# Layer 1's first eight columns of logits and v set among layer 0's last folds, and its contractions three columns later

## The chip, the cores and the metric

The kernel runs on one core of one Trainium2 chip. Its time is the device time of one execution, in microseconds (us); three runs are given for the kernel before. A profile is one more execution, recorded by the hardware profiler. The engines are TensorE (PE: matmuls; PEld: the loads of their stationary operand), VectorE (DVE), ScalarE (ACT), GpSimd (POOL) and SyncE (SP). SP computes nothing here and issues most transfers (DMAs); POOL and ACT issue some too. Every engine works through its instructions in the order in which the program lists them.

## The reference

Input x is [8, 56, 56, 384] in f32. Two layers follow one another, each of the form x = x + conv(gn(x)), where gn is a group norm with 32 groups without learned weights.

- Layer 0: v = gn(x) Wv. Each pixel has for each of 12 heads a 9 x 9 matrix of logits, a = gn(x) Wa, a softmax over its last axis, and with it makes 9 outputs out of the 3 x 3 neighbourhood of v; these are scattered back onto the 3 x 3 neighbourhood and added, and Wo is applied.
- Layer 1: logits gn(x) W_attn + b_attn (6 heads x 9), a softmax over the 9, v = gn(x) W_v + b_v, the weighted sum of the 3 x 3 neighbourhood of v, and W_proj with b_proj.

```
    y = jnp.einsum('bpKhd,bphK->bphd', patches, a)
    return y.reshape(B, H, W, C) @ W_proj + b_proj
```

## The kernel before

**Tiling.** Two images make a pair (4 pairs); a column is one x coordinate of a pair, 2 x 56 = 112 rows, with 384 channels. A pair has 56 columns, so layer 0 has 224 column steps. The 56 columns are cut into 8 patches of 7 columns (`PX = 7`, px in the names). In layer 1 a patch of a pair is a "group" g, 32 of them. Normalised tokens (xn) are held eight columns at a time. As 8 x 112 tokens are 7 tiles of 128, one column step in eight computes no logits.

**Layer 0** (`layer0`, L426). Step by step, `attend` (L611) makes a column's logits (three matmul groups `bank<-wa_t,xn`) and v (`bank<-wv_t,xn`). DVE subtracts the maximum, ACT takes the exponential; `normalise` (L684) and `presum` (L697) on POOL scale and partly sum the weights; `keep_v` (L640) has POOL store v to a table in DRAM (vtab). `fold` (L732), four steps later (`LAG`), finishes the sums with shift matmuls (`pw`), ACT and DVE writing them into four buffers (wts), and SP writes them to a weight table in DRAM (ztab). When a patch is complete, `fetch_v` and `fetch_z` read back v as vp and the weights as z in banded form, and `plan` (L800) enters jobs: contractions `pc<-z,vp` (two images, four parts each), evicted by ACT into yT, and six output projections `po<-yT,wo_t`. DVE adds the residual (x1t) and takes statistics of it; SP stores x1t to DRAM (x). Several jobs share one buffer po, so that a po directly behind another waits for DVE's addition.

**Layer 1** (`layer1`, L1015) does the like: `load` (L1036) fetches a group's x1t into one of five buffers (wide, z), `normed` (L1049) is ACT's normalisation into xn, `attend` (L1086) makes logits and v at once (`bank<-wc_t,xn`, 438 wide), added to their biases by DVE (lgt, v); its `store` has POOL write lgt to the group's tile at, and v to vtab. In the next group's columns, `weigh` (L1120) at column 3, `share` (L1128) at column 4 and `move` (L1136) at column 5 make the softmax on DVE and ACT, three shift matmuls (`pw<-at,shift`), ACT's copies and a write to ztab. `fetch` (L1172) reads z and vp and enters the group's jobs: contractions, and six po with DVE's addition of the residual and a transpose, and the output's DMAs.

**Order.** It is written out by hand. A `Jobs` queue (L358) holds (due step, job); every column step of either layer runs at most two of its jobs, one ahead of and one behind the step's matmuls. The last four steps of layer 0's loop (224 to 227) have only folds and jobs. The layer-1 loop (L1242) counts its own steps from `base`, the step at which layer 0's loop ended; at its step 0, `last` (L997) fetches and plans layer 0's last patch. `fetch` of group g - 2 stands at column 0 of group g, its jobs due three steps later.

**Buffers.** Layer 0's tiles (xr, xt, xin, xn, wa_t, wv_t and others) are in pools that are given up when `layer0` returns; layer 1's pools are laid over them, so that the first write to one of these waits for what last used that place. Layer 1's weights wc_t (L1070), loaded on POOL's queue, are such a tile.

Of the kernel before, what the change touches and what calls it, by code (L numbers as in the profile page):

```python
# [8 lines left out]
F32 = mybir.dt.float32  # L9
# [6 lines left out]
def two_outlook_layers(  # L16
# [80 lines left out]
    NTAB0, NTAB1 = 2, 3  # L97

# [327 lines left out]
    def layer0(late, pools):  # L426

        late_w = late.enter_context(tc.tile_pool(name="late0", bufs=1))
        io = pools.enter_context(tc.tile_pool(name="io0", bufs=2))
        work = pools.enter_context(tc.tile_pool(name="work0", bufs=2))  # L430
        fixed = pools.enter_context(tc.tile_pool(name="fixed0", bufs=1))
# [3 lines left out]
        def block_tile(pair, blk):  # L435
            t = io.tile([P, XB * NCH * R], F32, tag="xt", name=f"xt_{pair}_{blk}")
            return t[:, : XB * NCH * R].rearrange("p (m i r) -> p m i r", m=XB, i=NCH)
# [5 lines left out]
        xr_bufs = [io.tile([P, XB * C], F32, tag=f"xr{n}", name=f"xr_{n}", bufs=1) for n in range(2)]  # L443
# [6 lines left out]
        wts = fixed.tile([P, NWT, E0 * HEADS0 * PX], F32, name="wts0")  # L450
        xns = [fixed.tile([P, NCH, NTILE, P], F32, name=f"xn0_{n}") for n in range(2)]
# [34 lines left out]
        def blocks_in(flat, n, at=0):  # L486
# [14 lines left out]
            io.tile([P, XB, NCH, R], F32, tag="xin", name="xin_2", bufs=1),  # L501
# [22 lines left out]
        for blk in range(NBLK):  # L524
            if blk + NXR - 1 < NBLK:
                first_load(blk + NXR - 1)
            for i in range(NCH):
                for _ in stats_chunk(0, blk, i):
                    pass
            if blk == 1:  # L530
                wv_t = fixed.tile([P, NCH, C], F32, name="wv0_t")
                rows_of_channels(wv_t, wv0, sync)
# [29 lines left out]
        wa_t = fixed.tile([P, NCH, K * NL], F32, name="wa0_t")  # L562
# [15 lines left out]
        def load(g):  # L578
            pair, blk = divmod(g, NBLK)
            xins[g] = io.tile([P, XB, NCH, R], F32, tag="xin", name=f"xin_{g}", bufs=1)  # L580
            sync.dma_start(
                xins[g], xTs[pair][:, blk * XB : (blk + 1) * XB]
            )
# [345 lines left out]
        LAG = 4  # L929
        for step in range(NPAIR * W + LAG):  # L930
            folding = fold(*divmod(step - LAG, W)) if step >= LAG else iter(())
            turning = turned(step)
            summing = []

            def weigh():

                normal = 1 <= step < NPAIR * W + 1 and (step - 1) % SB < NTILE
                if 2 <= step < NPAIR * W + 2:
                    summing.append(presum(*divmod(step - 2, W)))
                    next(summing[0])  # L940
                if normal:
                    normalise(*divmod(step - 1, W))
                if normal and step % SB == NTILE:
                    share_out(*divmod(step - 1, W))
                for part in summing:
                    next(part)
                if normal and step % SB < NTILE:
                    share_out(*divmod(step - 1, W))
                if normal:
                    keep_v(*divmod(step - 1, W))  # L950

            def between(n):

                if n == 0:
                    next(turning, None)
                    weigh()
                    jobs.run(step, 1)
                elif n == 1:
                    if step % SB != NTILE:
                        next(folding, None)  # L960
                    next(turning, None)
                elif n == 2:
                    jobs.run(step, 1)
                    norms.run(step, 1)
                else:
                    for part in summing:
                        next(part)
                    if step % SB == NTILE:
                        jobs.run(step, 1)
                        next(folding, None)  # L970
                    next(folding, None)

            if step < NPAIR * W:
                attend(*divmod(step, W), between)
                upkeep(step)
            else:
                for n in range(K + 1):
                    between(n)
            flush()

            for lag, read, b in ((0, fetch_v, 0), (1, fetch_z, 0), (2, fetch_v, 1), (3, fetch_z, 1)):
                pair, c = divmod(step - LAG - PX - lag, W)
                if pair >= 0 and c % PX == 0 and c // PX < NPX:
                    px = c // PX
                    read(pair, px, b)
                    if lag == 1:
                        final = pair == NPAIR - 1 and px - NPX
                        ends = {-3: (8, 9, 9, 10, 10, 11), -2: (6, 7, 7, 8, 8, 9)}.get(
                            final, (7, 7, 8, 8, 9, 10)
                        )  # L990
                        second = (5, 6) if final == -2 else (6, 6)
                        plan(
                            pair, px, (step + 4, step + 5), [step + n for n in second],
                            [step + n for n in ends],
                        )

        def last(due):  # L997
            for b in range(IMG):
# [3 lines left out]
                NPAIR - 1, NPX - 1, (due + 4, due + 5), (due + 8, due + 8), [due + 9 + n for n in range(6)]  # L1002
            )

        return step + 1, last, late_w
# [9 lines left out]
    def layer1(pools, base, last_of_layer0, late_w):  # L1015
        vector, scalar, sync = (InOrder(e) for e in (nc.vector, nc.scalar, nc.sync))
        io = pools.enter_context(tc.tile_pool(name="io1", bufs=2, reuse_waits="tile"))
        work = pools.enter_context(tc.tile_pool(name="work1", bufs=2, reuse_waits="tile"))
        fixed = pools.enter_context(tc.tile_pool(name="fixed1", bufs=1, reuse_waits="tile"))
# [10 lines left out]
        def wide(n, pool, tag):  # L1030
            if n not in wides:
                wides[n] = pool.tile([P, NCH * T + SPARE], F32, tag=tag, name=f"wide_{n}", bufs=1)
# [3 lines left out]
        def load(g, queue=sync):  # L1036
            pair, px = divmod(g, NPX)

            if g % 5 == 3:
                t = wide(3, late_w, "xres")  # L1040
            elif g % 5 == 4:
                t = halves[3]
            else:
                t = wide(g % 5, io, f"x1t{g % 5}")
# [20 lines left out]
        load(0, nc.gpsimd)  # L1065

        NW = SX1 * K * ROW1
        wzs = [fixed.tile([R, NW + PX + 1], F32, name=f"wz1_{n}") for n in range(2)]
        NC1 = NA1 + C
        wc_t = fixed.tile([P, NCH, NC1], F32, name="wc1_t")  # L1070
        rows_of_channels(wc_t[:, :, :NA1], wa1, nc.gpsimd)
        rows_of_channels(wc_t[:, :, NA1:], wv1, nc.gpsimd)

        xns = [fixed.tile([P, NCH, SB, R], F32, name=f"xn1_{n}") for n in range(2)]
        normed(0, 0, PX)

        wo_t = fixed.tile([P, NCH, C], F32, name="wo1_t")
        by = io.tile([P, NR * 4 * QC], F32, tag="ot", name="wo1_by")
        by = by[:, : NCH * C].rearrange("p (i n) -> p i n", i=NCH)
        nc.sync.dma_start(by, wo1.rearrange("(i p) n -> p i n", p=P))  # L1080
        for i in range(NCH):
            sort_columns(wo_t, by, i, nc.gpsimd.tensor_copy)
# [3 lines left out]
        def attend(g, m):  # L1086
# [9 lines left out]
            lg = work.tile([P, NA1], F32, tag="lgt", name=f"lgt_{col}", bufs=4)  # L1096
            vector.tensor_add(lg, pa[:, :NA1], ba_t)
            v = work.tile([P, C], F32, tag="v", name=f"v_1_{col}", bufs=5)
# [12 lines left out]

        def at_of(g):

            if g not in lgs:
                lgs[g] = work.tile([R, PX, K2, HEADS1], F32, tag="at", name=f"at_1_{g}")
            return lgs[g]
# [3 lines left out]
        def weigh(g):  # L1120

            at = lgs[g]
            mx = work.tile([R, PX, HEADS1], F32, tag="mx", name=f"mx1_{g}")
# [4 lines left out]
        def share(g):  # L1128

            at = lgs[g]  # L1130
            den = work.tile([R, PX, HEADS1], F32, tag="den", name=f"den1_{g}")
# [4 lines left out]
        def move(g):  # L1136
# [12 lines left out]
            wz = wzs[g % 2]  # L1149
# [22 lines left out]
        def fetch(g, due):  # L1172
# [34 lines left out]
            def project_out(half, j):  # L1207
# [9 lines left out]
                if j == 0:  # L1217
                    fetch.ot = io.tile([P, NR * 4 * QC], F32, tag="ot", name=f"ot_{g}_{half}")
# [21 lines left out]

        NG = NPAIR * NPX
        for step in range((NG + 1) * PX):  # L1242
            g, m = divmod(step, PX)

# [5 lines left out]
            if step == 0:  # L1250
                last_of_layer0(base + step)
            if step == 4:
                for wz in wzs:
                    nc.gpsimd.memset(wz, 0.0)
            if g and m == first:
                weigh(done)
            if g and m == second:
# [8 lines left out]
            if g and m == moved:  # L1266
# [5 lines left out]
            if m == 1 and g + 1 < NG:  # L1272
                load(g + 1)
            if g > 1 and m == 0:
                while not clear_bands.done:
                    jobs.run(None, 1)
                fetch(done - 1, base + step + 3)
            if last and m == 4:
                fetch_v(done, 0)
                fetch(done, base + step + 1)  # L1280
            elif 0 < g < NG and m == 5:
                fetch_v(done, 0)
# [3 lines left out]
    with ExitStack() as late:  # L1286
        with ExitStack() as pools:
            last_of_layer0 = layer0(late, pools)
        with ExitStack() as pools:
            layer1(pools, *last_of_layer0)  # L1290
# [38 lines left out]
```

## Time and profile before

| | us |
|---|---|
| median of 3 runs | 3188.24 |
| lowest, highest | 3183.09, 3190.77 |
| the profiled execution | 3187.7 |
| its span, first to last instruction | 3185.5 |
| mean granted clock of PE | 0.989 of full |
| PE busy | 3065.3 |
| DVE busy | 2084.8 |
| POOL busy | 1654.2 |
| ACT busy | 1005.2 |
| first matmul with wc_t (layer 1's first logits) | at 2091.8 |

Lines of the profile name a source line, an engine, an operation, and out<-in by the names in the program. A helper issues all matmuls (L128) and most other operations (L143), so that lines are told apart by their tiles. A group "at 128x972" has 128 partitions and 972 elements in each. "Idle before <- X" is time in which the engine had nothing to run, and the instruction that ended it. The granted clock is the share of full speed that PE got. Matmuls of f32 are listed as two entries each, so that three matmuls make x6.

### The profile page before, as it was taken

To read this page: it belongs to the slowest core of one execution; us is meant where nothing else is said; L and a number is where in the kernel's file an instruction comes from. 1 tells how busy PE (TensorE), PEld (TensorE's weight loads), DVE (VectorE), ACT (ScalarE), POOL (GpSimd) and SP (SyncE) were. 2 spreads that over 40 slices of the span, in tenths; PEclk is the share of its full clock that TensorE was granted. 3 is DMA by queue.
4 is the path that set the end of the run, shared out by engine and by line. 5 is a ranking of instruction groups with operands and counts; after the bars stand their busy time and mean duration, and the time that the engine had idled before them with its cause. 6 is when DMAs were issued, how large, how long until landed. Compare 5 with 4: busy or idle time off the path is not lost. (4 is left out here: it accounts for less than half of the span.)

```text
span 3185.5 us, 72855 instructions
## 1 busy us (share of the span) xinstructions
PE 3065.3 (96%) x27640; PEld 2093.4 (66%) x27640; DVE 2084.8 (65%) x4942; ACT 1005.2 (32%) x2422; POOL 1654.2 (52%) x2759
## 2 busy tenths in 40 slices
PE   6899999999999999999999999989999999999997
PEld 5667766777776677776776666645666565656655
DVE  5777777777777777777777777635454555555454
ACT  4333333343333334333333333222222222222221
POOL 2765665655556565656566566544334344434431
PEclk8999999999999999999999999999999999999999
DMA  9799987899997899988888987889899988989897
GB/s 303 225 306 319 307 273 260 300 296 300 325 311 235 275 305 303 314 280 286 280 250 262 309 275 247 286 279 242 219 230 246 234 235 228 251 222 241 233 236 154
DMA packets 619842, 850.86 MB, mean 267 GB/s; under 512 B 264926, under 2 KB 496562, under 8 KB 611170
## 3 DMA queue, kind: packets, MB, share of 16 engines
q1 hardware_dynamic: 522322, 711.31, 73.7%
q0 software_dynamic: 63824, 116.90, 11.8%
q10 hardware_dynamic: 33344, 17.98, 2.1%
q8 instruction: 218, 3.57, 0.5%
q14 instruction: 134, 1.10, 0.1%
HBM read 514.86 MB, written 322.17 MB: 263 GB/s over the span
## 5 line engine op out<-in xcount | busy, mean ns | idle before, releaser
L128 PE MATMUL bank<-wa_t,xn 128*128 128x288 f32 x3528 | 967.8, 411 | 15.7 <-ACT xn L143 10.3
L128 PE MATMUL po<-yT,wo_t 128*128 128x448 f32 (+1 forms) x2304 | 817.0, 497 | 26.5 <-DVE x1t L143 19.4
L143 POOL TENSOR_TENSOR at<-at,d 128x972 f32<-128x972 f32 x196 | 441.2, 2251 | 714.8 <-DVE d L143 387.7
L128 PEld LDWEIGHTS bank<-wa_t,xn 128*128 128x128 f32 x3528 | 647.7, 191 | 226.2 <-issue 17.6
L128 PEld LDWEIGHTS po<-yT,wo_t 128*128 128x128 f32 x2304 | 433.6, 191 | 328.7 <-issue 195.8
L143 ACT ACTIVATE at<-at 128x972 f32<-128x972 f32 (+1 forms) x228 | 215.3, 944 | 997.1 <-DVE at L143 992.3
L1104 POOL DMA_DIRECT2D at<-lgt x392 | 204.8, 526 | 591.9 <-DVE lgt L143 580.8
L143 DVE TENSOR_REDUCE mx<-bank 128x36 f32<-128x324 f32 x588 | 284.8, 484 | 311.2 <-PE bank L128 309.3
L128 PE MATMUL bank<-wc_t,xn 128*128 128x438 f32 x1176 | 478.8, 543 | 5.1 <-DMA wc_t<-in_wv 5.1
L143 ACT COPY yT<-pc 128x294 f32<-128x294 f32 (+2 forms) x512 | 198.5, 405 | 804.9 <-PE pc L128 803.5
L128 PE MATMUL bank<-wv_t,xn 128*128 128x384 f32 x1176 | 414.5, 489 | 0.0
L128 PEld LDWEIGHTS pc<-z,vp 121*32 121x32 f32 (+1 forms) x17664 | 337.6, 120 | 111.9 <-issue 69.2
L128 PE MATMUL pc<-z,vp 121*32 121x49 f32 (+1 forms) x17664 | 374.2, 218 | 23.2 <-DMA z<-ztab 7.9
L128 PEld LDWEIGHTS bank<-wc_t,xn 128*128 128x128 f32 x1176 | 215.6, 191 | 180.9 <-issue 167.8
L143 DVE TENSOR_TENSOR at<-bank,mx 128x324 f32<-128x324 f32 x588 | 291.5, 496 | 31.0
L128 PEld LDWEIGHTS bank<-wv_t,xn 128*128 128x128 f32 x1176 | 220.8, 190 | 132.0 <-issue 9.3
L143 POOL DMA_DIRECT2D vtab<-v x476 | 289.5, 612 | 12.2 <-issue 6.8
L143 POOL TENSOR_TENSOR pre<-at,at 112x108 f32<-112x108 f32 (+1 forms) x440 | 236.5, 538 | 85.0 <-DMA at<-at 36.2
L143 DVE TENSOR_TENSOR lgt<-bank,ba_t 128x54 f32<-128x54 f32 x196 | 42.0, 214 | 308.7 <-PE bank L128 308.7
L333 POOL DMA_DIRECT2D vtab<-v x392 | 211.6, 544 | 16.0 <-issue 7.8
L143 DVE SCALAR_TENSOR_TENSOR wide<-po,bo_t,wide 128x448 f32<-128x448 f32 (+1 forms) x156 | 97.5, 625 | 167.4 <-PE po L128 167.3
L143 ACT ACTIVATE wts<-pre,inside 112x48 f32<-112x48 f32 (+4 forms) x672 | 179.3, 358 | 78.1 <-DMA ztab<-wts 66.2
(111 smaller groups left out, 2816.9 us busy)
## 6 DMA issues: line engine op xcount, KB each, us to landing
z<-ztab SPq DMA_DIRECT2D x64, 2352.0 KB
vp<-vtab SPq DMA_DIRECT2D x64, 1536.0 KB
vp<-vtab SPq DMA_DIRECT2D x64, 945.0 KB
xres<-xT SPq DMA_DIRECT2D x32, 1176.0 KB
ztab<-wts SPq DMA_DIRECT2D x336, 110.2 KB
vtab<-v POOLq DMA_DIRECT2D x108, 336.0 KB, 6.6
xin<-xT SPq DMA_DIRECT2D x52, 672.0 KB
xr<-in_x SPq DMA_DIRECT2D x50, 672.0 KB
```

The lines of the kernel that those rows point to most:

```text
L128: tc.keep_in_program_order(nc.tensor.matmul(*args, **kwargs))
L143: return lambda *args, **kwargs: tc.keep_in_program_order(op(*args, **kwargs))
L333: queue.dma_start(bass.AP(table.tensor, table.offset + first, [*([line * step, count] for step, count in rows_of or ((1, rows),)), *([[(R ...
L1104: nc.gpsimd.dma_start(at_of(g_of)[row : row + n, m_of].rearrange("r k h -> r (k h)"), lg[lo : lo + n])
```

## The change

Layer 1 becomes a generator that layer 0 starts and steps. Its buffers are handed over by name: the large tiles of layer 0 become "homes" that outlive it, and layer 1's tiles are slices of these (wc_t and the tiles lgt, v and at in xt and xin and xr; xn in xn; x of group 0 in xr, of group 1 in wa_t; layer 1's projection weights in wv_t). 40 steps before layer 0's last column step, x of group 0 and wc_t are loaded on POOL's queue; 7 to 5 steps before it, group 0 is normalised. At the last column step and in the four steps after it, 2, 1, 2, 2 and 1 columns of layer 1 (steps 1 to 7 and 9; step 8 has none) are computed among the folds and jobs, each with its stores at the end of the step. Layer 1's own loop starts with its step 10 (`AHEAD`), there loads x of group 2 and the projection weights and plans layer 0's last patch one or two steps closer than before. All fetches and jobs of a group are made by `of, turn`, three columns (`BEHIND`) after the columns that made them before; weigh, share and move stay where they were. The loop is three steps longer at its end. Of the buffers of x, those of group 2 and of groups 3 and 4 change places, and x of group 3 is loaded at column 4.

```diff
+    AHEAD, BEHIND = 10, 3
...
-        io = pools.enter_context(tc.tile_pool(name="io0", bufs=2))
+        xr_home = late_w.tile([P, 2 * XB * C], F32, name="xr_home")
+        xt_homes = [late_w.tile([P, XB * NCH * R], F32, name=f"xt_{n}") for n in range(2)]
+        xin_home = late_w.tile([P, XB * NCH * R], F32, name="xin_home")
+        xn_homes = [late_w.tile([P, NCH * SB * R], F32, name=f"xn_{n}") for n in range(2)]
+        wa_home = late_w.tile([P, NCH * K * NL], F32, name="wa0_t")
+        wv_t = late_w.tile([P, NCH, C], F32, name="wv_t")
...
+        ahead = layer1((xr_home, xt_homes, xin_home, xn_homes, wa_home, wv_t), late_w)
+        last_step = NPAIR * W - 1
+        first_of = {last_step - 40: 1, last_step - 7: 1, last_step - 6: 1, last_step - 5: 1}
+        columns = {last_step: 2, last_step + 1: 1, last_step + 2: 2, last_step + 3: 2, last_step + 4: 1}
+        stores = []
         for step in range(NPAIR * W + LAG):
+            for _ in range(first_of.get(step, 0)):
+                next(ahead)
+            more = iter(range(columns.get(step, 0)))
...
                     jobs.run(step, 1)
+                    if next(more, None) is not None:
+                        stores.append(next(ahead))
...
                     for part in summing:
                         next(part)
+                    while stores:
+                        stores.pop(0)()
...
             plan(
-                NPAIR - 1, NPX - 1, (due + 4, due + 5), (due + 8, due + 8), [due + 9 + n for n in range(6)]
+                NPAIR - 1, NPX - 1, (due + 3, due + 4), (due + 6, due + 6),
+                [due + n for n in (7, 8, 8, 9, 9, 10)],
             )
...
-        wc_t = fixed.tile([P, NCH, NC1], F32, name="wc1_t")
+        wc_t = xt_homes[0][:, : NCH * NC1].rearrange("p (i n) -> p i n", i=NCH)
...
+        load(0, nc.gpsimd)
+        rows_of_channels(wc_t[:, :, :NA1], wa1, nc.gpsimd)
+        rows_of_channels(wc_t[:, :, NA1:], wv1, nc.gpsimd)
+        yield
+        for m0, m1 in ((0, 3), (3, 5), (5, PX)):
+            normed(0, m0, m1)
+            yield
+        load(1, nc.gpsimd)
+        for step in range(1, AHEAD):
+            if step % SB == 0:
+                continue
+            if step == PX - 1:
+                normed(1, 0, 3)
+            yield attend(*divmod(step, PX))
+        normed(1, 3, PX)
+
+        pools, base, last_of_layer0 = yield
...
+        base -= AHEAD
...
-        for step in range((NG + 1) * PX):
+        for step in range(AHEAD, (NG + 1) * PX + BEHIND):
             g, m = divmod(step, PX)
+            of, turn = divmod(step - BEHIND, PX)
...
-            if step == 0:
+            if step == AHEAD:
                 last_of_layer0(base + step)
+                load(2)
...
-            if g > 1 and m == 0:
-                while not clear_bands.done:
-                    jobs.run(None, 1)
-                fetch(done - 1, base + step + 3)
-            if last and m == 4:
-                fetch_v(done, 0)
-                fetch(done, base + step + 1)
-            elif 0 < g < NG and m == 5:
-                fetch_v(done, 0)
+            if of > 1 and turn == 0:
+                assert clear_bands.done
+                fetch(of - 2, base + step + 3)
+            if of == NG and turn == 4:
+                fetch_v(NG - 1, 0)
+                fetch(NG - 1, base + step + 1)
+            elif 0 < of < NG and turn == 5:
+                fetch_v(of - 1, 0)
```

## The prediction

> **What bounds the kernel now.** The page first: busy time by engine, and the slices of the span.
>
> ```profile
> PE 3065.3 (96%) x27640; PEld 2093.4 (66%) x27640; DVE 2084.8 (65%) x4942; ACT 1005.2 (32%) x2422; POOL 1654.2 (52%) x2759
> PE   6899999999999999999999999989999999999997
> DMA  9799987899997899988888987889899988989897
> ```
>
> TensorE (PE) is busy for 3065 of 3185.5 us, so no more than 120 us is to be had without taking matmuls away. The slices show where those are missing: the start, slice 26 (counted from 0: 2071 to 2150 us), the end. Next I asked for busy time by stretch (columns: length, PE, PEld, DVE, ACT, POOL busy, granted clock, DMA share, GB/s):
>
> ```profile
> 2044.00:2112.00 68.00, 46.91 (x588) 28.05 (x587) 21.34 (x58) 10.25 (x24) 24.26 (x49) 0.85 1.02 358
> 2112.00:2150.00 38.00, 37.28 (x386) 21.48 (x385) 15.66 (x40) 12.39 (x29) 27.17 (x39) 1.00 0.59 181
> 2150.00:2166.00 16.00, 12.27 (x105) 7.68 (x103) 7.77 (x20) 3.35 (x7) 5.27 (x11) 0.79 1.00 253
> 2260.00:3060.00 800.00, 796.70 (x6117) 481.89 (x6112) 415.70 (x722) 199.06 (x582) 319.79 (x605) 1.00 0.90 236
> ```
>
> In layer 1's steady stretch PE idles 3.3 us of 800: nothing is left there. Between the layers it idles 21.1 + 0.7 + 3.7 = **25.5 us** of 122, at a lowered clock in two of the three stretches. PE's timeline there (start, length, operation, count, idle before and what ended it):
>
> ```profile
> 2048.28 4.09 PE L128 MATMUL po<-yT,wo_t 128*128 128x448 f32 x6 [3.19 <-DVE x1t L143]
> 2053.08 2.52 PE L128 MATMUL po<-yT,wo_t 128*128 128x448 f32 x6 [0.31 <-DVE x1t L143]
> 2056.32 1.96 PE L128 MATMUL po<-yT,wo_t 128*128 128x336 f32 x6 [0.72 <-DVE x1t L143]
> ...
> 2067.94 1.04 PE L128 MATMUL pc<-z,vp 121*32 121x49 f32 x56 [2.12 <-issue]
> 2068.91 1.14 PE L128 MATMUL pw<-pre,shift 112*112 112x120 f32 x4
> 2075.16 4.21 PE L128 MATMUL pc<-z,vp 121*32 121x49 f32 x192 [5.11 <-DMA z<-ztab]
> 2080.98 2.52 PE L128 MATMUL po<-yT,wo_t 128*128 128x448 f32 x6 [1.61 <-ACT yT L143]
> 2084.22 2.52 PE L128 MATMUL po<-yT,wo_t 128*128 128x448 f32 x6 [0.72 <-DVE x1t L143]
> 2091.84 4.42 PE L128 MATMUL bank<-wc_t,xn 128*128 128x438 f32 x6 [5.10 <-DMA wc_t<-in_wv]
> ```
>
> Six matmuls po of 448 take 2.42 us elsewhere, here 4.09 after the 3.19 us wait: idle PE is slowed afterwards. Losses of this kind: po 1.67, pw 1.14-0.57, pc 4.21-2.80, bank 4.42-2.37, and at 2158 pc 2.81-1.61 and bank 4.03-2.47: together **8.5 us**. So the transition loses 25.5 + 8.5 = 34.0 us. The wait of 5.10 us has a long root, in the table of waits and in the chain that ended last:
>
> ```profile
> POOL wc_t L269 <- DMA wo_by<-in_wo: 23.4, 1, 23.4
> 2064.70 11.79 DMA ztab<-wts
> 2077.98 4.67 DMA wo_by<-in_wo
> 2083.63 8.08 DMA wc_t<-in_wv
> ```
>
> Layer 1's weights wc_t can only be loaded when layer 0's pools are given up, behind layer 0's last ztab write.
>
> **The end of the kernel**, same view of PE:
>
> ```profile
> 3150.48 2.76 PE L128 MATMUL pc<-z,vp 90*64 90x56 f32 x84 [1.15 <-DMA z<-ztab]
> 3157.26 4.66 PE L128 MATMUL pc<-z,vp 90*64 90x56 f32 x84 [4.03 <-DMA vp<-vtab]
> 3162.31 14.74 PE L128 MATMUL po<-yT,wo_t 128*128 128x448 f32 x36 [0.39 <-ACT yT L143]
> ```
>
> From the last logits (end 3116.7) to PE's end, 3177.05, it idles 7.5 us (0.30, 0.52, 0.71, 0.40, 1.15, 4.03, 0.39) and loses 1.9 + 2.6 us to the clock: 12.0 us.
>
> **The change, part by part.** The matmuls stay the same in number; only waits can differ.
>
> *Removed:* the 5.10 us wait for wc_t. Its loads (0.79 and 0.76 us of POOL issue), x of group 0 (0.58) and its normalisation go into layer 0. On POOL's queue they stand among normalise and presum in pair 2, where POOL idles 2.8 to 2.9 us in each step; the 16-element memset ahead of x waits for PE's last transpose of xr (ends 1459.2), and POOL reaches it at about 1459.9. Six ACT normalisations lie beside an ACT that is 32% busy. The 1.85 MB meet a DMA share near 0.88 instead of 1.02: 0 to 6 us (1.85 MB at 300 GB/s, all of it waited for); I take 0.3, since z is fetched well before its use there. x of group 1 goes to the old wa_t, behind layer 0's last wa_t matmul (2040.5): POOL waits for none of it, as its next operation starts at 2041.1 anyway, 0.7 us later with the issue.
>
> *Added between the folds:* eight columns of 2.37 us among po, pw and pc, 19.0 us of PE work ahead of the contraction that waits for z today. From the end of the first po of px 5 (2044.5), the changed PE order up to pc of px 6, second image, start to start: 8 columns x 2.3, 2 po x 2.25, 3 po x 1.7, 5 pw x 0.5, pc 2.8, gaps 0.72 + 2.12: 36.1, so 2080.6. Its z goes out behind x1t's store, after 3 of these columns, 2 po and 2 pw, near 2059 (2056.9 today), and took 18.2 us: 2077. The 5.11 wait and the 3.19 are covered, so are 1.61 and 0.31; so is the stretch at 2150 (statistics spread between contractions, z fetched three columns later). If the cover failed, the 5.1 us and its clock loss would be back.
>
> A rule against it: the Trainium skill, "DMA: Bandwidth & Descriptors", section "Issuing engines are not separate DMA queues", says transfers from every issuing engine share the same 16 engines and interleave. So POOL's stores slow SP's z: 8 columns of 27 KB logits and about 247 KB v are 2.2 MB, at 380 GB/s 5.8 us, and z would come at 2083, a wait of over 2 us. By the rows, though, x of group 0 (1176 KB, POOL, 2058.7) leaves exactly this stretch, and only some five of the eight stores are out before z lands: net about nothing. I take 0 and keep 4 (wait and clock) for the range.
>
> *Left or new in the transition:* po directly after po waits for x1t: 0.72 + twice (0.72+0.72+0.60) = 4.8. The 2.12 "issue" wait, kept. Two new waits: SP issues x of group 2 behind both z of px 7 (about 9.4 MB from 2082, at 380 GB/s it lands near 2108), and ACT's normalisation of it stands ahead of the eviction of pc of px 7, which PE reaches near 2107 (2080.6 + pc 2.8 + po 11.9 + gaps 2.0 + 4 columns 9.2 + pw 0.8); on POOL the 4.04 us memset of z stands ahead of stores of logits that DVE's maximum needs, ahead of x1t. Either costs 0 to 6; they delay the same work, so I take 3.0 for both. Clock: 1.0. Sum 10.9. **Transition: 34.0 - 10.9 = 23.1 us gained.**
>
> *Contractions three columns later, steady.* Fetches come five instead of two columns after the weights' write: more slack. Softmax on DVE now falls in the po columns. Worst group (a skipped column): share takes 0.83+0.42+0.55 = 1.8 us, then the third po's addition ends 9.0 us after the logits' end; PE needs that buffer at 11.5. Slack 2.5 us; cost 0. Bounds: -3 (all the idle time goes) to +1 us for each of 31 groups.
>
> *The end.* After the last logits PE has both contractions of group 29 (2 x 2.76 = 5.5), then the shift matmuls of group 31. These need: POOL's second issue at +1.2, landing 5.1, reduction to share 0.79+0.55+0.52+0.83+0.42+0.55, handovers 0.5: +10.5. A **new wait of about 5.0 us**, in PE's order ahead of po of group 29, which hid it before. After it z and vp of group 31 are issued about 12 us before use, as po of 30 lies between: the 1.15 + 4.03 go. What follows the new wait is slowed. The skill's "TensorE: Matmul & The Clock Gate", Part 1, lets the clock drop after about 3.4 us idle and return after as long: 1.7 us lost. The rows disagree in size: 1.67 after 3.19 (below its limit), 2.05 after 5.10, 4.5 after 4.03. I take their mean, 2.7 (by the page the total below would be 1 us better). End: 5.0 + 2.7 + 1.1 small waits = 8.8; **12.0 - 8.8 = 3.2 us gained.**
>
> **Sum:** 23.1 + 3.2 - 0.3 = 26.0 us. The profiled execution: 3187.7 us with span 3185.5, so span 3159.5. It lies 0.5 us under the runs' median: 3188.24 - 26 = **3162.2 us**.
>
> **Rivals.**
> A, transfers set the pace: DMA share is 1.02 through 2044 to 2112. The compressed stretch must move 9 columns' stores more (2.5 MB) and x earlier, less 1.85 MB. If z of px 7 and x of group 2 come late by that, half the transition's gain stays: 23/2 + 3 = 14 us, 3174. For: the share; against: PE asks for z of px 7 only 24 us after its issue.
> B, slower: DVE becomes the bound in po columns. If share's 1.8 us is not hidden, 31 x 1.8 = 56, less 26: +30, 3218. It decides from 0.84 us a group on. For: DVE is in order and everything meets there; against: the slack of 2.5 us and 52% load (415.7 of 800).
> C, the change does nothing: the waits behind x of group 2, POOL's memset and the shift matmuls take the gain back, within 9 us of before.
>
> **How the numbers follow.** Likeliest 0.65, own range 3152 to 3172; A 0.20; C 0.07; B 0.08. The measurement tells about 0.3% (9.6 us). Faster: the likeliest and nearly all of A, 0.84; same 0.08; slower 0.08. Range 3150 (no new wait in the transition, steady idle gone) to 3180 (A with the 4 us and 6 us bounds).
>
> **What would show it.** Transition: no idle time on wc_t or z over 2 us between 2044 and 2115, granted clock near 1.00 there, PE idle in all some 10 us; pc of layer 1's group 0 begins with 18 instead of 14 columns done. End: one wait of about 5 us at pw, none at pc of group 31. Steady 800 us: PE idle still under 5 us. Wrong: idle before po from DVE in every group (B), or DMA waits at pc of px 7 and at xn (A).

## Result and the profile after

The changed kernel is slower: 3274.17 us (median of 6 runs, 3264.13 to 3282.6) against 3187.59 us for the kernel before in the same comparison. The ratio is 1.0266, interval [1.0241, 1.0292]. The forecast was 3162.2 us, range 3150 to 3180; of its three rivals none described what happened. The profiled execution has a span of 3278.2 us, 92.7 more than before.

The page first, the same views as before: busy time, and the slices of PE and DMA.

```profile
PE 3105.4 (95%) x27640; PEld 2111.9 (64%) x27640; DVE 2077.5 (63%) x4942; ACT 1014.6 (31%) x2426; POOL 1653.7 (50%) x2760
PE   6899999999999999999999999899899899989987
DMA  9799988889978899997898987987799789878986
```

PE has the same 27640 instructions and is busy 40 us longer: they ran slower, at a mean granted clock of 0.975 instead of 0.989. The dent of slice 26 stands at slice 25 (2049 to 2131 us), and there are new eights at slices 28, 31, 35 and 38. By stretch (length, then busy PE, PEld, DVE, ACT, POOL, granted clock, DMA share, GB/s):

```profile
2044.00:2112.00 68.00, 61.10 (x551) 35.40 (x550) 30.93 (x84) 12.34 (x36) 40.30 (x76) 0.95 1.02 358
2112.00:2150.00 38.00, 28.95 (x438) 15.95 (x438) 11.40 (x27) 7.28 (x15) 20.54 (x25) 0.87 0.84 225
2150.00:2166.00 16.00, 15.40 (x134) 9.74 (x134) 8.10 (x18) 5.79 (x17) 4.81 (x10) 1.00 0.95 295
2260.00:3060.00 800.00, 748.79 (x5441) 447.92 (x5437) 365.87 (x644) 182.67 (x514) 287.52 (x543) 0.95 0.85 211
```

The transition did get better (over the first three stretches together 105.5 us busy of 122, before 96.5). The loss is in the stretch that the prediction had costed at nothing: PE idles 51 us of 800 where it idled 3.3, at a clock of 0.95. The table of PE's waits for those 800 us (total, times, longest) names one cause:

```profile
PE pc L129 <- DMA vp<-vtab: 46.7, 14, 5.0
PE pc L129 <- DMA z<-ztab: 3.4, 1, 3.4
PE po L129 <- ACT yT L144: 1.2, 3, 0.4
```

Cut at two marks (the start of the shift matmuls of groups 5 and 29), the 92.7 us lie like this: up to the last logits of layer 0 +2.7 (in e1 below, 0.0); from there to group 5, -15.0 (261.9 to 246.9); **groups 5 to 29, +89.8** (777.0 to 866.8); from there to the end +15.2. About 8 us of the second and the last figure are only moved: in the changed order two po (3.6) and 132 contraction matmuls (4.3) that stood ahead of a group's shift matmuls stand behind them.

One late vp, in PE's timeline:

```profile
2328.06 0.82 PE L129 MATMUL pw<-xr_home,shift 112*112 112x126 f32 x6
2328.71 3.55 PE L129 MATMUL po<-yT,wv_t 128*128 128x336 f32 x12
2332.10 2.37 PE L129 MATMUL bank<-xt,xn 128*128 128x438 f32 x6
2334.40 2.71 PE L129 MATMUL pc<-z,vp 90*64 90x56 f32 x84
2341.88 1.53 PE L129 MATMUL pc<-z,vp 90*64 90x56 f32 x24 [4.77 <-DMA vp<-vtab]
2343.35 4.75 PE L129 MATMUL bank<-xt,xn 128*128 128x438 f32 x6
```

The first image's contraction finds its vp; the second image's waits 4.77 us, and the next logits take 4.75 instead of 2.47 us: 7 us for one late transfer. SP's timeline in the same place shows that it was not the transfer that was slow:

```profile
2307.37 0.34 SPq L144 DMA_DIRECT2D vp<-vtab  x1
2307.76 4.93 SPq L144 DMA_DIRECT2D z<-ztab  x4
2334.80 0.32 SPq L144 DMA_DIRECT2D vp<-vtab  x1
2335.22 8.84 SPq L144 DMA_DIRECT2D out<-ot  x8
```

SP stood still for 22.1 us between z and the second vp, although the first vp, of the same table, had gone out at 2307.37 and the buffer had been free since 2312.9 (the end of the last matmul that reads it). It went on when something else landed, which ACT's timeline shows:

```profile
2328.91 0.99 ACT L144 COPY wz<-pw 112x42 f32<-112x42 f32 x9 [13.86 <-PE pw L129]
2329.93 0.31 ACTq L144 DMA_DIRECT2D ztab<-wz  x1
```

That is the write of the *next* group's weights. The vp needs nothing of it. But in the records of the trace each transfer names the semaphore (a counter that engines wait on) that it raises when it lands, and over SP's and ACT's transfers these run through eight numbers in turn (100 to 107 in the records, here 0 to 7). In the built program each transfer first waits until the one that had its number before has landed. At 2334.80 the vp has number 3; the write at 2329.93 has number 3 too. SP's records show the wait itself: it is for number 3, the write's landing makes the last of its 16 updates of that number at 2334.74, and SP goes on at 2334.76.

SP's numbers also show where the write was counted. The outputs ahead of z run 4, 5, 6, 7, 0, 1, 2 and then 4 again: the missing 3, between 2304.84 and 2305.71, is the write's, and eight places on stands the vp. In the source that fetch (column 3) still comes ahead of the write (column 5). So the order in which the numbers were given is not the order of the source; why, no run here shows. The writes of eight groups in a row, with the transfer of SP that was held after each, from the records of the trace:

```
group  write of ztab  its number   SP held, until       its number   group's period
  5       2292.0          3        vp    2296.7             3             37.9
  6       2329.9          3        vp    2334.8             3             39.7
  7       2369.6          3        vp    2374.9             3             37.7
  8       2407.3          4        out   2412.1             4             31.8
  9       2439.1          4        out   2449.4             4             32.5
 10       2471.6          4        out   2483.4             4             35.6
 11       2507.2          4        out   2519.0             4             32.5
 12       2539.7          2        z     2546.3             2             42.0
```

For all 28 writes of groups 3 to 30 the transfer that has the number next goes out at most 0.1 us (once 0.4) after the last update of that number. The pattern repeats about every eight groups, in step with the one column in eight that has no logits. Some four periods in eight are slow, 6.5 us above the 32 to 34 us of the kernel before. In that kernel the ninth transfer, counting the write as the first, is the first vp *of the same group* in nearly all groups (write at 2304.24, vp at 2308.94, both number 5). That vp does not need the write, but z stands directly behind it (2309.34) and does, so the shared number costs nothing. With the fetches three columns later, the ninth transfer is the second vp, or z, of the group *before* the write's, or an output.

### The profile page after: what moved, and what is told of

It is laid out like the page before. It is cut to its first block, busy times and chain, and to the rows that moved or that the text cites. A ratio compares the mean times of both kernels' runs of the same rounds, so it can differ in the third digit from the quotient of the medians.

```text
span 3278.2 us, 72810 instructions
## 1 busy us (share of the span) xinstructions
PE 3105.4 (95%) x27640; PEld 2111.9 (64%) x27640; DVE 2077.5 (63%) x4942; ACT 1014.6 (31%) x2426; POOL 1653.7 (50%) x2760
## 3 DMA queue, kind: packets, MB, share of 16 engines
q14 instruction: 133, 1.09, 0.1%
## 5 line engine op out<-in xcount | busy, mean ns | idle before, releaser
L129 PE MATMUL bank<-xt,xn 128*128 128x438 f32 x1176 | 506.9, 569 | 6.3 <-issue 6.3
L144 ACT ACTIVATE at<-at 128x972 f32<-128x972 f32 x196 | 198.7, 1014 | 948.9 <-DVE at L144 948.5
L129 PE MATMUL po<-yT,wo_t 128*128 128x336 f32 (+1 forms) x1152 | 416.8, 498 | 15.7 <-DVE x1t L144 15.7
L129 PE MATMUL po<-yT,wv_t 128*128 128x336 f32 (+1 forms) x1152 | 396.1, 495 | 2.4 <-ACT yT L144 2.4
L129 PEld LDWEIGHTS bank<-xt,xn 128*128 128x128 f32 x1176 | 225.9, 200 | 189.0 <-issue 170.7
L129 PEld LDWEIGHTS po<-yT,wv_t 128*128 128x128 f32 x1152 | 216.8, 191 | 162.1 <-issue 112.2
L129 PEld LDWEIGHTS po<-yT,wo_t 128*128 128x128 f32 x1152 | 215.0, 193 | 148.5 <-issue 75.5
L144 POOL DMA_DIRECT2D vtab<-v x476 | 289.5, 612 | 13.8 <-issue 6.2
L1120 POOL DMA_DIRECT2D xr_home<-xt x147 | 76.9, 526 | 270.7 <-DVE xt L144 244.1
L1120 POOL DMA_DIRECT2D xin_home<-xt x147 | 76.9, 526 | 249.8 <-DVE xt L144 242.4
```

Source lines behind the costliest of these rows:

```text
L129: tc.keep_in_program_order(nc.tensor.matmul(*args, **kwargs))
L144: return lambda *args, **kwargs: tc.keep_in_program_order(op(*args, **kwargs))
L1120: nc.gpsimd.dma_start(at_of(g_of)[row : row + n, m_of].rearrange("r k h -> r (k h)"), lg[lo : lo + n])
```

## Experiments

Theory S: the shared numbers make the loss. Theory T: the delay bunches outputs, x, vp and z, and the data engines deliver vp late. "Held by the count" is read off the built program for the writes of groups 3 to 30: which transfer of SP has the number that this write had before it. "None" means that only transfers stand there which follow the write anyway.

| run | median us | ratio to before | held by the count | PE busy of the 800 us |
|---|---|---|---|---|
| before | 3187.6 | 1 | none | 796.7 |
| changed | 3274.2 | 1.0266 | vp 10, z 4, then outputs | 748.8 |
| e1: changed, ztab from SP | 3177.1 | 0.9957 | none | 798.2 |
| e2: before, later by 3 | 3269.1 | 1.0249 | vp 4, else outputs | 758.7 |
| e3: before, ztab from SP | 3192.0 | 1.0005 | none | 798.2 |
| e4: changed, x from ACT | 3215.3 | 1.0083 | vp 4, else outputs | 781.7 |
| e5: e2, ztab from SP | 3193.8 | 1.0009 | none | 798.0 |
| e6: changed, later by 4 | 3195.2 | 1.0023 | z 26, vp 2 | 786.8 |
| e7: e6, ztab from SP | 3173.2 | 0.9954 | none | 798.2 |
| e8: e1, last pc spread | 3172.7 | 0.9953 | none | 798.2 |
| e9: changed, softmax a column earlier | 3207.9 | 1.0043 | z 27, vp 1 | 783.3 |
| e10: changed, softmax a column later | 3205.2 | 1.0043 | outputs | 779.3 |
| e11: e7 and e8 | 3170.5 | 0.9932 | none | 798.2 |

**e1.** The write of ztab goes to SP's own queue.

```diff
-            scalar.dma_start(
+            sync.dma_start(
                 bass.AP(
                     table.tensor, table.offset + MARGIN * LINE1 + FIRST1 * ROW1,
```

> The changed kernel, with layer 1's write of ztab issued from SP's queue instead of ACT's, in the same place of the program; nothing else is moved, all transfers stay. Theory S (shared semaphores): the transfers of SP and ACT take eight completion semaphores in turn, and each first waits until the transfer eight places before it has landed; in the changed kernel the transfer eight places before vp (or z) of group g is, in 14 groups, the ztab write of group g + 1, a whole group later. From SP's own queue the write stands ahead only of transfers that follow it anyway: the 14 waits of about 7 us go (14 x 6.9 = 97 us), 3274 - 97 = 3177 us (3165 to 3190), and PE waits for no vp for over 1 us between 2260 and 3060. Theory T (traffic: out, x, vp and z are issued in one burst and vp lands late): the same bytes in the same order, so 3274 us within 10, the waits of 4 to 5 us at pc stay.

Measured 3177.06 us, ratio 0.9957 [0.9943, 0.9971]. PE's waits in the 800 us:

```profile
PE po L129 <- ACT yT L144: 1.2, 3, 0.4
PE pc L129 <- ACT yT L144: 0.6, 3, 0.2
```

and SP's timeline:

```profile
2312.20 3.50 SPq L144 DMA_DIRECT2D out<-ot  x4
2315.91 0.41 SPq L144 DMA_DIRECT2D ztab<-wz  x1
2319.85 3.48 SPq L144 DMA_DIRECT2D out<-ot  x4
2323.37 0.72 SPq L144 DMA_DIRECT2D wide<-x  x1
2324.33 0.56 SPq L144 DMA_DIRECT2D vp<-vtab  x1
2324.99 6.37 SPq L144 DMA_DIRECT2D z<-ztab  x4
2331.46 4.52 SPq L144 DMA_DIRECT2D vp<-vtab  x1
```

All 97 us of the loss are gone with one word, at a DMA share of 0.93 instead of 0.85: more traffic per microsecond, and no late vp. Theory T falls.

**e3.** The same edit in the kernel before, as a control.

> The kernel before, with layer 1's ztab write on SP's queue instead of ACT's. A control: in the kernel before, the write stands eight places before vp of its own group, which needs it anyway, so theory S gives 3188 us within 8. If the queue itself matters (ACT's issue, or SP being held up by the wait for ACT's copies), the time moves by over 10 us here too.

3192.0 us, ratio 1.0005 [0.9995, 1.0015]. The queue alone is worth nothing; it matters where the shared number does harm.

**e2.** The kernel before with the three columns' delay only.

```diff
-        for step in range((NG + 1) * PX):
+        for step in range((NG + 1) * PX + BEHIND):
             g, m = divmod(step, PX)
+            of, turn = divmod(step - BEHIND, PX)
```

> The kernel before, with its layer-1 contractions, fetches and projections three columns later and nothing else of the change. Theory S: counted through the program, the ztab write of the next group stands eight places before vp of the second image in groups 3, 11, 19 and 27 alone (in the others before an output's transfer, which is later anyway): 4 x 6.9 = 28 us, so 3188 + 28 = 3216 us (3200 to 3232), PE periods of a group of 38 to 39 us where the four waits are and 32 us elsewhere. Theory T: every group has the same burst, 30 x 3.3 = 100 us, about 3290 us.

3269.11 us, ratio 1.0249 [1.0232, 1.0266]: the delay alone costs 78 us, so the eight columns among the folds are not the cause. That the time is near the changed kernel's is chance: there 97 us are lost and some 14 to 21 gained. But S had said 3216. The waits:

```profile
PE pc L129 <- DMA z<-ztab: 25.0, 15, 3.9
PE pc L129 <- DMA vp<-vtab: 14.6, 9, 3.9
```

The four slow periods of 39 to 42 us are where the count had them, but two more are 39.2 and 40.5 us, and many of the rest 33 to 37. There an output is held, and behind it in SP's queue are x, vp and z:

```profile
2409.68 24.69 SPq L144 DMA_DIRECT2D out<-ot  x8
2434.47 0.49 SPq L144 DMA_DIRECT2D wide<-x  x1
2435.19 0.34 SPq L144 DMA_DIRECT2D vp<-vtab  x1
2435.58 4.94 SPq L144 DMA_DIRECT2D z<-ztab  x4
```

The eight outputs take 24.69 us here, and the next vp and z go out at 2435; in the changed kernel the same groups' outputs take 8.54 us and z goes out at 2423.2, 20 us ahead of its use. So S had the right cause, and was wrong in holding an output to be harmless; the next run tests that.

**e5.** e2 with the write on SP's queue.

> The kernel before with contractions three columns later (as in the run before, 3269 us), and layer 1's ztab write on SP's queue instead of ACT's. Theory S, mended: a write of ztab eight places before an output's transfer also does harm, since SP keeps the next x, vp and z behind it; all of the 78 us come from the shared semaphores and go: 3188 us within 10, PE idle in the 800 us from 2260 on under 5 us. Theory T (part of the 78 us is the delay's own burst of transfers): at least 20 us of it stay, over 3208 us.

3193.76 us, ratio 1.0009 [0.9998, 1.0019]. All of e2's loss came from the shared numbers. By itself, a delay of three columns costs nothing that can be told from the noise: the prediction's "cost 0" is true of the fetches and false of the queue that they stand in.

**e4.** x of the later groups from ACT's queue; ztab stays on ACT, so that only the places change.

```diff
-                load(g + 1)
+                load(g + 1, scalar)
```

> The changed kernel, with the loads of x of groups 4 and later issued from ACT's queue instead of SP's, and the ztab write left on ACT. Theory S: by the count, the wait is left at vp of groups 3, 11, 19 and 27 alone, 4 in place of 14: 3274 - 10 x 6.9 = 3205 us (3190 to 3222). Theory T: same bytes at the same times, 3274 us within 10; if it is x standing ahead of vp on SP's queue that makes vp late, all waits go and the time is near 3177 us.

3215.31 us [1.0065, 1.0100], as S had it to 10 us. The slow periods are 37.8, 39.9, 40.6 and 39.2 us, at the writes of groups 4, 12, 20 and 28: the four that the count names. This rules out that e1 helped only because ACT was relieved of a transfer.

**e6 and e7.** Four columns' delay instead of three, with ztab from ACT and from SP.

```diff
-    AHEAD, BEHIND = 10, 3
+    AHEAD, BEHIND = 10, 4
```

> The changed kernel with its contractions four instead of three columns later, ztab written from ACT's queue. By the count, the ztab write of group g + 1 now stands eight places before z of group g in every group from 3 on, 28 in place of 14. Theory S: 28 x 7 = 196 us above the 3177 us without such waits: 3373 us (3320 to 3410), every group near 39 us. Theory T, or the plain reading that a column more gives the transfers more time: not slower than 3274 us.

> As the run with four columns, with ztab written from SP's queue. Theory S: as with three columns, 3177 us within 8; a delay of one column more costs nothing by itself. If the delay has a price of its own, some 10 us or more above 3177.

e7 came as expected, 3173.21 us. e6 gave 3195.21 us [1.0014, 1.0033] where 3373 was expected: twice as many held transfers, a fifth of the loss (22 us against e7). PE's waits in the 800 us, in a profiled execution that was its fastest (3181.8 us):

```profile
PE pc L129 <- DMA vp<-vtab: 11.5, 11, 1.5
```

SP is held in every group here too, but it is asked for later. In the changed kernel the write lets vp go 6.5 to 7.1 us after the start of the shift matmuls, vp takes 7.0 more, some 13.8 in all, and PE asks for it after 9.1 to 11.6 us. In e6 the first two are nearly the same (6.6 to 7.5 in all but two groups, and 7.2 to 7.6), and PE asks after 13.2 to 15.7 us. So a held transfer has no price of its own: it costs what it comes later than its user asks. This reading was made after e6; e9 tests it.

**e9 and e10.** Softmax, shift matmuls and write one column earlier, and one later.

```diff
-            first, second, moved = (1, 2, 3) if last else (3, 4, 5)
+            first, second, moved = (1, 2, 3) if last else (2, 3, 4)
```

> The changed kernel with weigh, share and move of every group one column earlier (columns 2, 3, 4), ztab written from ACT's queue; contractions three columns later as they are. By the count, the ztab write of group g + 1 stands eight places before z of group g in 28 groups. If each such wait had one price (7 us), 3177 + 28 x 7 = 3373 us. If its price is the time by which vp, issued when that write has landed, comes later than PE asks for it (5 us where the shift matmuls stand 9 us before the second image's contractions; near 1 us in the run with four columns, where they stand 13 us before), a column more between them makes it as in that run: 3195 us (3180 to 3210).

> The changed kernel with weigh, share and move one column later (columns 4, 5, 6), ztab written from ACT's queue. The write lands one column later in every group, but by the count it stands eight places before an output's transfer in all groups, before vp or z in none until the last. Theory S with places: the 14 late vp and z go, 3180 us (3168 to 3196), although everything that the write feeds is later. Theory with the landing alone (the later the write, the later what follows it): over 3274 us. Theory T: 3274 us.

e9 leaves out the maximum, subtraction and exponential of group 0, some 2 us beside PE's work. It gave 3207.92 us [1.0027, 1.0058], inside its range: with a column more between write and use, 28 held transfers cost 11.1 us of waiting for vp in the 800 us, none over 1.8. e10 gave 3205.15 us [1.0028, 1.0059] and was missed: a later write is indeed better here than the changed kernel, by 69 us, which no theory of landing times alone allows. But the outputs that it holds are again not free (waits of 7.0 us for z and 4.6 for vp, and 7.7 for ACT's eviction).

**e8 and e11.** In the changed kernel PE stops twice in layer 0's last patches, waiting for nothing that the profile names. e8 takes e1 and spreads the last contractions over two columns:

```diff
-                NPAIR - 1, NPX - 1, (due + 3, due + 4), (due + 6, due + 6),
+                NPAIR - 1, NPX - 1, (due + 3, due + 4), (due + 5, due + 6),
```

> The changed kernel with ztab written from SP's queue (3177 us), and the second image's contractions of layer 0's last patch made 96 and 96 in two columns instead of 192 in one. In the changed kernel PE stops for 5 to 6 us some two microseconds after these 192, in the middle of a group of three matmuls, waiting for nothing that the profile names; a block of 16 KB on the instruction queue lands 1 to 2 us before it goes on. If this is PE's program arriving late behind data transfers (each of the 192 matmuls brings a weight load, and these are short), spreading them shortens the stop to under 2 us: 3173 us. If the stop has another cause, it stays and the time is 3177 us.

3172.67 us [0.9936, 0.9969], against 3177.06 [0.9943, 0.9971] for e1. The intervals overlap, so the gain is not shown. The stop of 5.18 us was cut up, not removed:

```profile
2125.26 0.50 PE L129 MATMUL pc<-z,vp 121*32 121x49 f32 x23 [3.18 <-issue]
2134.08 1.66 PE L129 MATMUL po<-yT,wo_t 128*128 128x448 f32 x4 [1.38 <-issue]
```

> The changed kernel with ztab written from SP's queue, contractions four columns later, and the last contractions of layer 0 as 96 and 96: the two edits that gave 3173.2 and 3172.7 us together. Both act on other places (the start of group 0's contractions, PE's stops in layer 0's last patch), so at most 3177 - 4 - 4 = 3169 us; if the differences of 4 us were only scatter, 3175 us within 4.

3170.46 us, ratio 0.9932 [0.9920, 0.9944]. This version, with the write on SP's queue, four columns and the spread contractions, is faster than both kernels: 0.7% under the kernel before, 3.2% under the changed one.

## Why the prediction was wrong

**Contractions three columns later, steady: the step that failed.** It said "Fetches come five instead of two columns after the weights' write: more slack", took the cost as 0, and bounded it at +1 us for each of 31 groups; even these 31 us were left out of its range, which they would have taken to 3193. Measured: 97 us in all (changed against e1), +89.8 us of them in 24 groups. The step looked at which data a fetch needs and at DVE. It did not ask what else SP waits for before each fetch, and so missed the wait for the next group's write. The lines to find it by were there. SP's waits in the kernel before, 2300 to 2900, begin with one on a transfer of ACT's queue, once in nearly every group:

```profile
SPq L143 <- DMA ztab<-wz: 168.9, 18, 12.0
```

and the same stretch in the changed kernel:

```profile
SPq L144 <- DMA ztab<-wz: 299.1, 16, 24.3
```

Before, it looks like a plain wait for data. That every ninth transfer is tied to the first whatever its data is, only the semaphore numbers in the trace's records and the wait lists of the built program show.

**Rivals.** B (DVE the bound) has no trace: PE's waits on DVE in the 800 us are none. A (transfers set the pace) was to show at pc of px 7 and at xn, and did not; e1 moves the same bytes at a higher share. C supposed waits in the transition. All had been drawn from the engines' load and the bytes; the cause was an order.

**Transition: right in mechanism, mis-sized.** Compared in e1, where the steady loss is out of the way. Its stretches:

```profile
2044.00:2112.00 68.00, 61.48 (x646) 35.93 (x644) 30.58 (x81) 12.12 (x37) 39.03 (x76) 0.97 1.03 367
2112.00:2150.00 38.00, 28.54 (x350) 16.42 (x351) 11.40 (x27) 7.31 (x16) 19.63 (x24) 0.91 0.88 217
```

No wait for wc_t or z is left between 2044 and 2115, and layer 1's first contraction begins with 18 columns done, 14 before, both as said. The po gaps are 4.8 us, as said. The new wait for ACT's eviction is 2.77 + 0.46 us, for 3.0. The 4 us that were kept for the range, for data engines shared with POOL's stores, did not come: no wait for z there, so the 0 taken was right. The mis-sized terms are two. "Issue" was kept at 2.12; it is 2.89 + 0.49 + 5.18 = 8.6. The clock was put at 1.0; on the busy time it is 61.48 x 0.03 + 28.54 x 0.09 = 4.4. With the idle 6.5 + 9.5 + 0.6 the residual is 21.0 instead of 10.9, the gain 13.0 instead of 23.1; by the marks used above it is 20.5 - 7.9 = 12.6. The loads inside layer 0, put at 0.3 us, cost nothing that e1 shows: layer 0's last logits end at 2040.5 there as before.

**End: the sign right, the new wait too large.** Predicted: 5.0 us at the shift matmuls of group 31. In e1:

```profile
3103.30 0.56 PE L129 MATMUL pc<-z,vp 90*64 90x56 f32 x12 [0.44 <-ACT yT L144]
3104.89 0.91 PE L129 MATMUL pw<-xin_home,shift 112*112 112x126 f32 x6 [1.02 <-DVE xin_home L144]
```

The chain took 7.3 instead of 10.5 us, mostly since the last store of logits landed 2.2 us after its issue (3098.65 to 3100.80), not 5.1. The trace of the kernel before could have told: 5.1 is the median of these stores over the whole of layer 1, but its last two (3117.3 and 3117.8) landed after 2.3 and 2.0 us. The waits for vp shrank to 1.09 and 0.75 from 4.03. By the marks the end gained 0.9 + 7.9 = 8.8 us, predicted 3.2. So without the steady loss the sum would have been 21 us in the profiled executions (3185.5 to 3164.3), and 14 in the medians (3191.2 to 3177.1); predicted 26. That 21 comes near 26 is in part luck: 10 us too much for the transition and 6 too little for the end offset each other.

**The clock.** A wait of 3.22 us in the changed kernel is followed by logits of 4.31 us instead of 2.47. So a wait shorter than the 3.4 us that the Trainium skill ("TensorE: Matmul & The Clock Gate", Part 1) names was followed by a loss of 1.8 us. The rows were the better guide. What the prediction missed was the sum: 13 waits of 2 to 5 us, none in the same group as another, stand in the 800 us whose clock fell to 0.95 (51 us idle there), and over the whole kernel PE's matmuls take 40 us longer.

## What to carry to other kernels

When a transfer is moved in the program's order, read in the built program which transfer it waits for, not only which data. Here completion semaphores taken in turn tie a fetch to whatever was counted eight places before it, and across two issuing queues that can be something much later in time. Such a tie costs nothing where the transfers behind the follower need the earlier one anyway (e3); elsewhere it costs as much as the follower, or what stands behind it, then comes later than its user asks. Putting the odd write on the queue whose transfers follow it took the whole loss away here (e1, e5, e7); shifting the count by a place (e4, e10) took away a part. A delay "with more slack" is to be costed on the queue it joins, with everything behind it.

## What the runs showed of the hardware

PE also stops for what looks like its own program arriving in blocks. The trace has 217 or 218 transfers of 16 KB on an instruction queue in every run, and each long stop marked "issue" in the transition ends 1.3 to 1.6 us after such a block has landed:

```
kernel   block lands   PE goes on   stop before
before     2066.51      2067.94        2.12
e1         2082.26      2083.76        2.89
e1         2130.13      2131.51        5.18
e6         2124.63      2126.22        2.35
```

That the blocks are PE's program is inferred from these times; the trace does not say whose they are. The stops come in or behind runs of 192 short matmuls, each with its own weight load. Why the block at 2129.06 came 8.5 us after the one before it in e1, and the one at 2123.61 only 6.5 us after its own in e6, was not settled. The data engines' load does not tell the two apart: between the two blocks their share was 1.05 in e1 and 1.06 in e6. No run varied one thing alone there.
